# A two-layer graph network on one core: the first group as four tasks, and a new order of steps around the change of layers and in the second layer

## The chip, the cores and the metric

The kernel runs on one core of a Trainium2 chip. The metric is the time of one execution on the device in microseconds (us). Before the change three runs took 2112.41, 2112.71 and 2116.83 us; the median is 2112.71 us. One more execution was profiled.

## The reference

There are 128 graphs of 128 nodes with 512 features, all in float32. Two layers follow each other, each with a residual and a layer norm. Cut to what is computed:

```python
# layer 0, per graph
deg = sum(adj, -1); agg = (adj @ x) / max(deg, 1e-6)
x = layernorm(x + relu(concat([x, agg]) @ W.T))
# layer 1, per graph
Xw = x @ Wv + bv; e = leaky_relu(sj(Xw)[None, :] + si(Xw)[:, None] + ab, 0.2)
T = adj * exp(e);  T = T / (sum(T, -1) + 1e-12)
H = x @ Wk[0] + bk[0] + (T @ x) @ Wk[1] + bk[1] + (T @ T @ x) @ Wk[2] + bk[2]
x = layernorm(x + relu(H))
```

## The kernel before

**Groups and products.** Four graphs make a group, so the left operand of a group has 512 rows and 512 features; there are 32 groups (`NG`) in each layer. The adjacency is applied after the weights: the first layer computes `x @ W` for both halves of `W` and then multiplies one half by the normalised adjacency, and the second layer does the same with the weights of the three hops and two extra columns for the scores. The big product is done by a scheme that needs seven block products where the plain one needs eight, twice nested. One outer product (called 1 to 7) is a sequence of seven inner products of 128x128 by 128x256 (first layer) or 128x385 (second layer). The sums of blocks that it needs are made on the left operand (`x_inner`, `x_s1` to `x_s4`, tiles `xu`, `xl`, `xs`) and on the weights (`w_inner`, `w_outer`, the tile `big`). A matmul in float32 appears in the profile as two MATMUL instructions, called passes here.

**Tasks and steps.** A task is a Python generator that yields after each step; a step issues one inner product (in the first layer's paired tasks two) and what belongs to it. `P12`, `P56`, `P74` and `T` make a group of the first layer, `O1` to `O7` and the combination `C` one of the second. Tasks run on two lanes of four PSUM banks, `bA` and `bB`. Within an outer product, X, Y, W and Z are the four banks of its lane. Step 1 writes X, which ScalarE copies to Y (L617 in the second layer); step 2 writes Z, which is copied to the tile s5 (L623, or L621 with a bias); step 3 adds into X, and VectorE writes W = X + s5 (L626); in adding tasks POOL adds to s5 (L660); step 4 adds into Y, which is evicted (L647 on ScalarE, L656 on VectorE); step 5 adds into X, and VectorE takes X + s5 as a result (L650 or L663); step 6 adds into W, which is evicted; step 7 adds into X once more, which is evicted last. So step 3 waits for the copy of step 1, step 5 for the add of step 3, and step 7 for the direct add of step 5. `O5` starts with a copy of the bias to X (L615).

**The order.** The order of all instructions on every engine is written out by hand. The lists `PA`, `PT`, `PB` and `PL` name the steps of a group of the first layer, of the change of layers, of a group of the second layer and of the last group; a name in small letters belongs to the group before. `PB` is used for all groups of the second layer but the last, the first from its `O5.1` on. Everything that is no step (loads, turns, sums, layer norm, softmax) is an operation with a place: a number in half steps, relative to the start of its group, in `PLACES_A` (first layer), `PLACES_B` (second layer), `PLACES_M` and `PLACES_L` (the end), `PLACES_T` (loads of the second layer's weights) and `START`. An even place is after the step's own instructions, an odd one after its late evictions. Each engine works through its list in order, and SyncE (SP) issues nearly all transfers in order.

**The first group.** At the start the derived weights do not exist yet. The task `first` computes group 0 with 56 inner products in 14 steps of four matmuls, two columns (o = 0, 1), and each step uses both halves of the left operand (`xu`, `xl`). The constants of the second layer's bias and scores are folded (`fold_constants`) between these steps, with the loaded `wvt` in the buffers of the tile `y`. `first_last` (FL) multiplies by the adjacency.

**Layer norm.** The last products of a group are followed by the residual on VectorE (L371), the mean on POOL (`ln_mean`, L488), four squares on ScalarE (`ln_var`, L493), the scales on POOL (`ln_scales`, L499 to L501) and four applications on ScalarE (`ln_apply`, L506).

Of the kernel before, what the change touches and what calls it, by code (L numbers as in the profile page):

```python
# [8 lines left out]
FP = mybir.dt.float32  # L9
# [7 lines left out]
def kernel(  # L17
# [14 lines left out]
    nc = tc.nc  # L32
# [9 lines left out]
    R = 32  # L42
# [67 lines left out]
    wvt_sb = [p2.tile([P, 2, F], FP, name=f"wvt{i}", tag="y") for i in range(2)]  # L110
# [3 lines left out]
    bk_sb = p1.tile([K, F], FP, name="bk_sb", tag="TT")  # L114
# [5 lines left out]
    load_w0([nc.scalar], 1)  # L120
    load_w0([nc.scalar], 3)
    load_adj(0)
    for i in range(2):
        nc.sync.dma_start(wvt_sb[i], wvt[i * FH : (i + 1) * FH, :].rearrange("(c p) f -> p c f", p=P))
# [32 lines left out]
    def fold_constants():  # L157
        ones_row = ones[:].to_broadcast([P, P])
        pb, pc, pw = bB[0], bB[3], bB[0]
# [17 lines left out]
        w2row = p1.tile([2, NC, Q, R], FP, name="w2row", tag="TT")  # L177
# [79 lines left out]
    def x_inner(n, p):  # L257
        need(("x_turn", n, p, 1))
        t = (xu, xl)[p][n]
        left_sums([S_, S_, S_, S_], [t[:, :, i] for i in range(7)])  # L260
# [71 lines left out]
    def p12(lane, g):  # L332
        r, c11 = rs[g], c11s[g] = blocks(p2, "r"), blocks(p2, "c11")

        def evict(b, t):
            L_.copy(part(r, b), t[:, :FH])
            V.tensor_add(part(c11, b), t[:, FH:], part(r, b))
        yield from pair(lane, g, 1, 2, evict)
# [10 lines left out]
    def p74(lane, g):  # L349
        r, c22, c21 = rs[g], blocks(p2, "c22"), blocks(p2, "c21")  # L350
        c22s[g], c21s[g] = c22, c21

        def evict(b, t):
            need(("P56", g, {BY: 4, BWW: 6, BZ: 7, BX: 7}[b]))
            L_.copy(part(c22, b), t[:, :FH])
            V.tensor_add(part(c21, b), t[:, FH:], part(r, b))
            V.tensor_add(part(c21, b), t[:, :FH], part(c21, b))
        yield from pair(lane, g, 7, 4, evict)
# [68 lines left out]
    def first(lane, g):  # L427
        c11, c21 = blocks(p2, "c11"), blocks(p2, "c21")
        c11s[g], c21s[g] = c11, c21

        def column(o, bank_of, evict):
            X, Y, W, Z = [bA[i] for i in bank_of]

            def prod(dst, k, start=False):
                for h in range(2):
                    for i in range(2):
                        mm(dst[:, h * FH : (h + 1) * FH], (xu, xl)[h][g][:, i, LEFT[k]], wf[:, SLOT[2 * i + o], RIGHT[k]],
                           start and i == h == 0)
            s5 = halves()
            prod(X, 1, True)  # L440
            L_.copy(Y, X)
            yield
            prod(Z, 5, True)
            L_.copy(s5, Z)
            yield
            prod(X, 6)
            V.tensor_add(W, X, s5)
            yield
            prod(Y, 2)
            yield  # L450
            prod(X, 7)
            evict(BY, Y)
            V.tensor_add(Z, X, s5)
            yield
            prod(W, 3)
            yield
            prod(X, 4)
            evict(BWW, W)
            evict(BZ, Z)
            late.append((evict, BX, X))  # L460
            yield

        def evict0(b, t):
            L_.copy(part(c11, b), t[:, :FH])
            V.tensor_copy(part(c21, b), t[:, FH:])
        yield from column(0, (0, 1, 2, 3), evict0)

        def evict1(b, t):
            i, h = b
            L_.copy(bB[i][:, h * FH : (h + 1) * FH], t[:, :FH])  # L470
            V.tensor_copy(bB[2 + i][:, h * FH : (h + 1) * FH], t[:, FH:])
        yield from column(1, (1, 2, 0, 3), evict1)
        lane[:] = [bA[2], bA[3], bA[1], bA[0]]

    def first_last(lane, g):
        new_mv(g)
        for p, t in ((1, c21s[g]), (0, c11s[g])):
            for i in range(2):
                b = 2 * p + i
                mm(bB[b], aTs[g][:, b], t[:, i, :, :FH])  # L480
                late.append((residual, g, b, bB[b]))
            yield
        lane[:] = [bB[2], bB[0], bB[1], bB[3]]
# [326 lines left out]
    TASKS = {"F": first, "FL": first_last, "P12": p12, "P56": p56, "P74": p74, "T": last, "O1": o1, "O2": o2, "O5": o5,  # L810
             "O6": o6, "O7": o7, "O4": o4, "O3": o3, "C": combine}
    lanes = [list(bA), list(bB)]
    steps = []

    def step(lane, name, g, k):
        steps.append((lane, name, g, k))

    PA = "p74.5 P12.1 P12.2 p74.6 P12.3 p74.7 P12.4 t.1 P12.5 P12.6 t.2 P12.7 P56.1 t.3 P56.2 t.4 t.5 P56.3 t.6 t.7 t.8 t.9 t.10 t.11 P74.1 P74.2 P56.4 P56.5 P56.6 P74.3 P56.7 P74.4".split()
    PT = "p74.5 O1.1 O1.2 p74.6 O1.3 O1.4 p74.7 t.1 t.2 O1.5 O1.6 O1.7 O2.1 t.3 O2.2 t.4 t.5 O2.3 t.6 t.7 t.8 t.9 t.10 t.11 O2.4 O2.5 O2.6".split()
    PB = ("o3.7 O1.1 O1.2 O2.1 O1.3 O2.2 O1.4 O1.5 O1.6 O1.7 O2.3 O2.4 O5.1 O5.2 O2.5 O5.3 O5.4 O2.6 O5.5 "  # L820
          "O2.7 O6.1 O5.6 O6.2 O5.7 O7.1 O6.3 O7.2 O6.4 O6.5 O7.3 O6.6 O6.7 O7.4 O4.1 O7.5 O4.2 O7.6 O4.3 "
          "O7.7 O4.4 O4.5 O4.6 c.1 O4.7 O3.1 c.2 O3.2 O3.3 O3.4 c.3 c.4 c.5 c.6 c.7 c.8 O3.5 O3.6").split()
# [3 lines left out]
    for k in range(14):  # L826
        step(0, "F", 0, k + 1)
# [18 lines left out]
    for g in range(NG):  # L846
        base[NG + g] = base[NG] + len(PB) * g
        for s in PB[PB.index("O5.1") if g == 0 else 0 :] if g < NG - 1 else PL:
# [16 lines left out]
    def place(n, pos, f, *a):  # L865
        at(2 * base[n] + pos, f, *a)

    PLACES_A = {
# [9 lines left out]
        ("y_store", 0, 1): 280, ("ln_var", 0, 2): 229, ("sum_r", 0, 1): 77, ("load_adj", 0): 129, ("ln_apply", 0, 0): 245,  # L878
        ("ln_apply", 0, 3): 257, ("ln_var", 0, 1): 229, ("load_y", 0, 0): 163, ("x_s2", 1): 71, ("ln_var", 0, 3): 233,
        ("t_load", 0): 125, ("x_turn", 1, 0, 0): 14, ("t_turn", 0): 189, ("sum_r", 0, 0): 85, ("x_turn", 1, 0, 1): 33,  # L880
        ("y_store", 0, 0): 258, ("load_y", 0, 1): 183, ("ln_apply", 0, 2): 270, ("ln_var", 0, 0): 231, ("t_back", 0): 158,
        ("t_exp", 0): 140, ("x_s4", 0): 43, ("ln_mean", 0): 224, ("sum_c", 0, 1): 106, ("ln_scales", 0): 233,
        ("sum_c", 0, 0): 114, ("t_sums", 0): 150, ("x_s3", 1): 84, ("x_s1", 1): 69, ("load_left", 2, 0): 66,
        ("x_turn", 1, 1, 0): 2, ("t_scores", 0): 116, ("t_norm", 0): 151, ("x_inner", 1, 0): 38, ("x_inner", 1, 1): 25,
        ("load_left", 2, 1): 38, ("x_turn", 1, 1, 1): 12, ("ln_apply", 0, 1): 256,
# [20 lines left out]
    for n in range(2 * NG):  # L906
        for (name, dn, *a), pos in (PLACES_A if n < NG else PLACES_B).items():
# [6 lines left out]
            place(n, pos, OPS[name], m - NG if name in OWN else m, *a)  # L914
# [10 lines left out]
    def fold(i):  # L925
        next(folding, None)
# [9 lines left out]
    def w_outer(i):  # L936
        need(("w_inner", 1), *{1: [], 2: [("w_outer", 1)], 3: [("F", 0, 14)], 4: [("w_outer", 2)]}[i])
# [4 lines left out]
        ("w_inner", 1): 9, ("x_s2", 1): 30, ("fold", 2): 3, ("a_turn", 0): 16, ("w_outer", 2): 16, ("fold", 4): 11,  # L942
        ("degree", 0): 10, ("a_norm", 0): 10, ("load_left", 1, 1): 9, ("x_s1", 1): 21, ("fold", 5): 16, ("fold", 3): 8,
        ("w_outer", 1): 11, ("fold", 7): 10, ("fold", 6): 17, ("x_s3", 1): 22, ("w_outer", 4): 19, ("load_y", 0, 0): 17,
# [72 lines left out]
```

## Time and profile before

| what | value |
|---|---|
| median of three runs | 2112.71 us |
| the profiled execution's own time | 2111.64 us |
| its span, first to last instruction | 2109.8 us |
| TensorE busy | 2083.5 us, 7104 MATMUL |
| VectorE, ScalarE, POOL busy | 1464.6, 1145.5, 1539.4 us |
| TensorE idle before the second product of the start | 4.1 us, on the turn of `xl` |
| a group of the first layer | about 24.65 us |
| a group of the second layer | 39.5 us |

The profile comes from one execution. Busy time of TensorE counts every matmul to its modelled end, and matmuls overlap, so a short pause between two of them need not appear as idle time; the distance from start to start tells more. A line of the timeline gives the start, the time from there to the end of the last of the merged instructions, the engine, the line of the source, the operation, its tiles and its shape, how many were merged, and in brackets how long the engine was idle before and what ended that.

### The profile page before, as it was taken

What the parts mean: (1) busy time and instruction counts of PE and PEld (TensorE: products, weight loads), DVE (VectorE), ACT (ScalarE), POOL (GpSimd) and SP (SyncE); (2) the same over time, 40 slices, a digit from 0 to 9 for tenths busy, and PEclk for the clock granted to TensorE, in tenths of its full rate; (3) what the DMA queues carried; (4) which work ended last, traced back from release to release, by engine and by line L of the source; (5) the groups of instructions that cost most, each with busy time, mean ns of one, the idle gap of its engine ahead of it and who ended that gap; (6) DMA issues with size and microseconds to landing.
All of it is one profiled execution on the core that took longest, in us unless ns stands there. A gap on an engine that the chain in (4) does not pass through costs nothing.

```text
span 2109.8 us, 25967 instructions
## 1 busy us (share of the span) xinstructions
PE 2083.5 (99%) x7104; PEld 1328.1 (63%) x7104; DVE 1464.6 (69%) x3235; ACT 1145.5 (54%) x2879; POOL 1539.4 (73%) x1432
## 2 busy tenths in 40 slices
PE   8999999999999999999999999999999999999997
PEld 5887888888778886555555555555555555555553
DVE  4778777777777776666666666666666666666665
ACT  2665666666656665355455455455455455455454
POOL 5877888887767776767767767767767767767763
PEclk9999999999999999999999999999999999999999
DMA  7766666566566768334434434434434434434423
GB/s 177 183 186 190 189 184 173 159 190 192 160 173 182 191 164 239 76 91 121 109 91 119 112 91 121 109 91 120 111 91 120 111 91 120 111 91 121 110 71 115
DMA packets 429486, 287.13 MB, mean 136 GB/s; under 512 B 153497, under 2 KB 352281, under 8 KB 429340
## 3 DMA queue, kind: packets, MB, share of 16 engines
q1 hardware_dynamic: 428092, 283.62, 50.7%
q10 hardware_dynamic: 1120, 1.84, 0.4%
q8 instruction: 56, 0.92, 0.2%
q14 instruction: 90, 0.74, 0.1%
q0 software_dynamic: 128, 0.01, 0.0%
HBM read 191.60 MB, written 93.79 MB: 135 GB/s over the span
## 4 chain that ended last, share of the span: by engine, by line
PE 95%; DVE 2%; POOL 1%; DMA 1%; ACT 1%; issue 0%; ACTq 0%; SPq 0%; POOLq 0%; DVEq 0%
PE bB L149 50%; PE bA L149 45%; DVE y L371 1%; DVE r L663 1%; DMA xb<-in_x_dram 0%; DMA big<-wd 0%; DMA big<-in_w0t_dram 0%; PE bB L174 0%; POOL s L660 0%; ACT junk L493 0%; POOL r L696 0%; ACT T L762 0%; POOL xs L265 0%; POOL xs L269 0%; POOL xu L277 0%
## 5 line engine op out<-in xcount | busy, mean ns | idle before, releaser
L149 PE MATMUL bA<-big,xu 128*128 128x256 f32 (+1 forms) x1834 | 578.6, 435 | 3.3 <-DVE r L663 1.0
L149 PEld LDWEIGHTS bA<-big,xu 128*128 128x128 f32 x1834 | 345.6, 190 | 177.6 <-issue 25.7
L149 PE MATMUL bB<-big,xl 128*128 128x256 f32 (+1 forms) x1330 | 399.1, 416 | 0.2 <-ACT bB L617 0.2
L149 PE MATMUL bA<-big,xs 128*128 128x256 f32 (+1 forms) x1316 | 387.9, 418 | 0.2
L149 PEld LDWEIGHTS bB<-big,xl 128*128 128x128 f32 x1330 | 252.0, 190 | 99.3 <-issue 15.5
L149 PEld LDWEIGHTS bA<-big,xs 128*128 128x128 f32 x1316 | 245.1, 190 | 92.1 <-DVE bA L626 14.3
L149 PE MATMUL bB<-big,xu 128*128 128x256 f32 (+1 forms) x868 | 286.1, 440 | 2.6 <-DVE bB L388 2.5
L149 PE MATMUL bB<-c,TT 128*128 128x512 f32 x512 | 246.3, 594 | 0.0
L660 POOL TENSOR_TENSOR s<-s,r 128x385 f32<-128x385 f32 x128 | 127.6, 997 | 151.2 <-DVE bA L626 105.3
L493 ACT ACTIVATE junk<-y,mv 128x512 bf16<-128x512 f32 x252 | 181.6, 721 | 78.6 <-POOL mv L488 74.5
L149 PEld LDWEIGHTS bB<-big,xu 128*128 128x128 f32 x868 | 159.0, 189 | 91.7 <-DVE r L650 19.3
L506 ACT ACTIVATE y<-y,mv,rstd 128x512 f32<-128x512 f32 x252 | 201.4, 811 | 1.3 <-POOL mv L501 1.3
L626 DVE TENSOR_TENSOR bA<-bA,s 128x385 f32<-128x385 f32 x128 | 72.5, 567 | 165.6 <-ACT s L623 117.8
L149 PE MATMUL bA<-big,xl 128*128 128x385 f32 (+1 forms) x490 | 181.3, 476 | 4.2 <-DVE xl L254 4.1
L371 DVE SCALAR_TENSOR_TENSOR y<-bB,y 128x512 f32<-128x512 f32 x256 | 170.4, 682 | 19.8 <-PE bB L149 13.5
L149 PE MATMUL bB<-big,xs 128*128 128x385 f32 x448 | 173.5, 492 | 0.9 <-POOL xl L242 0.9
L149 PEld LDWEIGHTS bB<-c,TT 128*128 128x128 f32 x512 | 97.2, 190 | 89.4 <-issue 48.6
L797 ACT COPY bB<-r 128x512 f32<-128x512 f32 x64 | 37.7, 589 | 193.4 <-DVE big L796 188.2
L277 POOL TENSOR_TENSOR xu<-xu,xs 128x896 f32<-128x896 f32 x63 | 131.3, 2085 | 10.3 <-PE bA L149 10.3
L149 PEld LDWEIGHTS bA<-big,xl 128*128 128x128 f32 x490 | 93.3, 191 | 71.0 <-DVE c L663 7.9
L273 POOL TENSOR_TENSOR xl<-xu,xl 128x896 f32<-128x896 f32 x63 | 133.3, 2116 | 1.1
L269 POOL TENSOR_TENSOR xs<-xs,xu 128x896 f32<-128x896 f32 x63 | 131.7, 2090 | 2.4
(172 smaller groups left out, 3540.3 us busy)
## 6 DMA issues: line engine op xcount, KB each, us to landing
xb<-in_x_dram SPq DMA_DIRECT2D x256, 128.0 KB, 3.5
y<-in_x_dram SPq DMA_DIRECT2D x64, 512.0 KB, 4.5
yd<-y SPq DMA_DIRECT2D x64, 512.0 KB, 2.8
xb<-yd SPq DMA_DIRECT2D x256, 128.0 KB, 3.9
y<-yd SPq DMA_DIRECT2D x64, 512.0 KB, 4.4
out_dram<-y SPq DMA_DIRECT2D x62, 512.0 KB, 2.8
ag<-in_adj_dram SPq DMA_DIRECT2D x64, 256.0 KB, 4.0
sb<-sd SPq DMA_DIRECT2D x252, 64.0 KB, 3.1
```

The source lines that it names most:

```text
L149: nc.tensor.matmul(dst, lhsT, rhs, start=start, stop=True, skip_group_check=True)
L269: S_.tensor_sub(xs[n][:, 1], xs[n][:, 0], xu[n][:, 0])
L273: S_.tensor_sub(xl[n][:, 0], xu[n][:, 0], xl[n][:, 0])
L277: S_.tensor_sub(xu[n][:, 1], xu[n][:, 1], xs[n][:, 1])
L371: V.scalar_tensor_tensor(y, t, 0.0, y, ALU.max, ALU.add, accum_out=mvs[n][:, b, 0:1])
L493: L_.activation(junk, ys[n, b // 2][:, b % 2], AF.Square, bias=mvs[n][:, b, 0:1], accum_out=mvs[n][:, b, 1:2])
L506: L_.activation(y, y, AF.Identity, bias=mvs[n][:, b, 0:1], scale=rstds[n][:, b : b + 1])
L626: V.tensor_add(W, X, s5)
L660: S_.tensor_add(s5, s5, part(src, BZ, BW))
L663: V.tensor_add(part(dst, BZ, BW), X, s5)
L797: L_.copy(at_[b], row(b, 254, 766, 1))
```

## The change

- The first group is computed by four tasks A to D, one for each column o and half h of the left operand, with seven steps of two products each. A uses `xu` alone and the weights 0 and 2. Each works in halves of four banks (A and B in `bA`, C and D in `bB`); C and D evict to `bA`. Their order is the list `PF`. The turns of `xl` and its sums move to places among these steps, and the inner sums of group 0 go from POOL to VectorE.
- The loads of the weights 1 and 3 are shared by the queues of ScalarE and SyncE. `wvt` is loaded from step 16 on, into the buffers of `c22`. The folding of the constants moves to steps 38 to 51, beside group 1, in banks of `bA`. All places of `START` are new. The lanes start with exchanged banks.
- `PT` is new; the first group of the second layer has its own list `PG`; the others but the last have a new `PB`. `PLACES_B` and `PLACES_T` are new.
- Operations of the last two groups of the first layer and the first two of the second take their places from a new table `PLACES_S`, counted from the start of `PT`.

```diff
-    load_w0([nc.scalar], 1)
-    load_w0([nc.scalar], 3)
+    load_w0([nc.scalar, nc.sync], 1)
+    load_w0([nc.scalar, nc.sync], 3)
     load_adj(0)
...
-        pb, pc, pw = bB[0], bB[3], bB[0]
+        need(("FL", 0, 2))
+        pb, pc, pw = bA[2], bA[3], bA[2]
...
-        left_sums([S_, S_, S_, S_], [t[:, :, i] for i in range(7)])
+        left_sums([S_ if n else V] * 4, [t[:, :, i] for i in range(7)])
...
+    def first(g, o, h):
+        X, Y, W, Z = [t[:, h * FH : (h + 1) * FH] for t in (bA, bB)[o]]
+        if o == 0:
+            dst = blocks(p2, "c21" if h else "c11")
+            (c21s if h else c11s)[g] = dst
+        else:
+            need(("w_inner", 1))
+
+        def prod(dst, k, start=False):
+            for i in range(2):
+                mm(dst, (xu, xl)[h][g][:, i, LEFT[k]], wf[:, SLOT[2 * i + o], RIGHT[k]], start and i == h == 0)
+
+        def evict(b, t):
+            if o == 0:
+                to = part(dst, b)
+            else:
+                need(("FA", 0, 7), ("FB", 0, 7))
+                to = bA[2 * h + b[0]][:, b[1] * FH : (b[1] + 1) * FH]
+            if (b[0] + b[1]) % 2:
+                L_.copy(to, t)
+            else:
+                V.tensor_copy(to, t)
+        s5 = halves()[:, :FH]
...
+        prod(X, 7)
+        V.tensor_add(Z, X, s5)
+        yield
+        prod(W, 3)
+        late.append((evict, BWW, W))
+        yield
+        prod(X, 4)
+        late.append((evict, BZ, Z))
+        late.append((evict, BX, X))
+        yield
...
+    PF = "A.1 A.2 A.3 A.4 A.5 A.6 B.1 B.2 B.3 C.1 B.4 A.7 C.2 B.5 C.3 B.6 B.7 C.4 C.5 C.6 D.1 D.2 D.3 D.4 D.5 D.6 C.7 D.7".split()
-    PT = "p74.5 O1.1 O1.2 p74.6 O1.3 O1.4 p74.7 t.1 t.2 O1.5 O1.6 O1.7 O2.1 t.3 O2.2 t.4 t.5 O2.3 t.6 t.7 t.8 t.9 t.10 t.11 O2.4 O2.5 O2.6".split()
-    PB = ("o3.7 O1.1 O1.2 O2.1 O1.3 O2.2 O1.4 O1.5 O1.6 O1.7 O2.3 O2.4 O5.1 O5.2 O2.5 O5.3 O5.4 O2.6 O5.5 "
-          "O2.7 O6.1 O5.6 O6.2 O5.7 O7.1 O6.3 O7.2 O6.4 O6.5 O7.3 O6.6 O6.7 O7.4 O4.1 O7.5 O4.2 O7.6 O4.3 "
-          "O7.7 O4.4 O4.5 O4.6 c.1 O4.7 O3.1 c.2 O3.2 O3.3 O3.4 c.3 c.4 c.5 c.6 c.7 c.8 O3.5 O3.6").split()
+    PT = "p74.5 p74.6 O1.1 O1.2 O1.3 p74.7 O1.4 t.1 O1.5 O1.6 t.2 O1.7 O2.1 t.3 O2.2 t.4 t.5 O2.3 t.6 t.7 t.8 t.9 t.10 t.11 O2.4 O2.5 O2.6".split()
+    PG = ("O5.1 O5.2 O5.3 O5.4 O2.5 O2.6 O6.1 O6.2 O5.5 O5.6 O5.7 O7.1 O6.3 O6.4 O7.2 "
+          "O6.5 O2.7 O7.3 O6.6 O7.4 O6.7 O4.1 O4.2 O7.5 O4.3 O7.6 O7.7 O4.4 c.1 O4.5 "
+          "O4.6 c.2 c.3 c.4 O4.7 O3.1 O3.2 O3.3 O3.4 c.5 c.6 c.7 c.8 O3.5 O3.6").split()
+    PB = ("O1.1 o3.7 O1.2 O1.3 O2.1 O2.2 O1.4 O1.5 O1.6 O1.7 O2.3 O2.4 O5.1 O5.2 O5.3 O2.5 O2.6 O5.4 O5.5 "
+          "O2.7 O6.1 O5.6 O6.2 O5.7 O7.1 O6.3 O7.2 O6.4 O6.5 O7.3 O6.6 O6.7 O7.4 O4.1 O4.2 O7.5 O4.3 O7.6 "
+          "O4.4 O7.7 O4.5 c.1 c.2 O4.6 O4.7 O3.1 O3.2 c.3 c.4 O3.3 c.5 O3.4 c.6 c.7 c.8 O3.5 O3.6").split()
...
+    def place_op(n, pos, name, m, *a):
+        key = name, m - NG, *a
+        if name not in OWN and key in PLACES_S:
+            at(2 * start_b + PLACES_S[key], OPS[name], m, *a)
+        else:
+            place(n, pos, OPS[name], m - NG if name in OWN else m, *a)
+
+    PLACES_S = {
+        ("ln_apply", -2, 3): 4, ..., ("ln_apply", -2, 2): 10, ..., ("ln_apply", -2, 1): 15, ..., ("ln_apply", -2, 0): 15,
+        ("ln_var", -1, 0): 58, ..., ("ln_scales", -1): 62, ("ln_mean", -1): 48, ("ln_var", -1, 2): 55, ...
+        ("x_inner", 1, 1): 61, ("x_inner", 1, 0): 64, ("x_s4", 0): 80, ("x_s1", 1): 97, ("x_s2", 1): 99, ("x_s3", 1): 127,
+        ...
+    }
...
     PLACES_B = {
-        ("ln_apply", 0, 2): 270, ..., ("ln_apply", 0, 3): 257, ..., ("load_left", 2, 0): 66, ("load_left", 2, 1): 38,
+        ("ln_apply", 0, 2): 274, ..., ("ln_apply", 0, 3): 255, ..., ("load_left", 2, 0): 83, ("load_left", 2, 1): 59,
...
     START = {
+        ("x_turn", 0, 1, 0): 6, ("x_turn", 0, 1, 1): 8, ("x_inner", 0, 1): 13, ("w_inner", 1): 16, ("w_outer", 1): 22,
+        ("load_wvt",): 32, ("a_load", 0): 35, ("a_turn", 0): 59, ("fold", 1): 77, ..., ("fold", 7): 102, ...
```

## The prediction

> **What bounds the kernel now.** I read the page first, then the stretches, TensorE's waits, and the timeline of the start, of the change of layers and of one steady group of the second layer. The page and three stretches (us, then busy us and instructions of PE, PEld, DVE, ACT, POOL, then clock, DMA share, GB/s):
>
> ```profile
> span 2109.8 us, 25967 instructions
> PE 2083.5 (99%) x7104; PEld 1328.1 (63%) x7104; DVE 1464.6 (69%) x3235; ACT 1145.5 (54%) x2879; POOL 1539.4 (73%) x1432
> 0.00:20.00 20.00, 13.21 (x29) 7.31 (x30) 6.84 (x11) 1.85 (x2) 10.14 (x26) 0.91 0.99 216
> 800.00:845.00 45.00, 41.41 (x140) 25.65 (x138) 28.29 (x64) 23.65 (x53) 27.17 (x31) 1.00 0.85 242
> 1100.00:1500.00 400.00, 399.16 (x1153) 213.19 (x1152) 262.79 (x545) 206.09 (x509) 290.05 (x263) 1.00 0.42 107
> ```
>
> TensorE sets the time. Its visible idle time is 26.3 us: most of it in the first 20 us and near 820 us, next to nothing in steady stretches. Its longest waits (total, times, longest):
>
> ```profile
> PE bA L149 <- DVE xl L254: 4.1, 1, 4.1
> PE bB L149 <- DVE bB L388: 2.5, 1, 2.5
> PE bB L149 <- POOL xl L242: 0.9, 1, 0.9
> ```
>
> Busy hides the rest, because a matmul's shown end is modelled. What counts is the distance between starts. A product is two MATMULs; where nothing holds it, four starts of 385 columns take 1.29 us, 0.646 per product. One steady group (start, duration):
>
> ```profile
> 1134.18 2.45 PE L149 MATMUL bA<-big,xu 128*128 128x385 f32 x6
> 1135.09 0.56 DVE L663 TENSOR_TENSOR r<-bA,s 128x385 f32<-128x385 f32 x1
> 1136.46 1.46 PE L149 MATMUL bB<-big,xu 128*128 128x385 f32 x4
> 1137.31 0.46 ACT L617 COPY bB<-bB 128x385 f32<-128x385 f32 x1 [0.22 <-PE bB L149]
> 1139.69 3.02 PE L149 MATMUL bB<-big,xu 128*128 128x385 f32 x8
> 1142.55 1.46 PE L149 MATMUL bA<-big,xu 128*128 128x385 f32 x4
> 1143.29 0.49 ACT L615 COPY bB<-beta 128x385 f32<-128x385 f32 x1
> 1143.92 1.53 PE L149 MATMUL bB<-big,xs 128*128 128x385 f32 x4
> 1145.29 0.81 PE L149 MATMUL bA<-big,xu 128*128 128x385 f32 x2
> 1153.70 1.59 PE L149 MATMUL bA<-big,xs 128*128 128x385 f32 x4
> 1155.13 0.81 PE L149 MATMUL bB<-big,xl 128*128 128x385 f32 x2
> 1171.07 2.81 PE L149 MATMUL bB<-big,TT 128*128 128x512 f32 x6
> 1173.71 2.44 PE L149 MATMUL bA<-big,xu 128*128 128x385 f32 x6
> ```
>
> The group takes 1173.71 - 1134.18 = 39.53 us; its work is 49 x 0.646 + 8 x 0.858 = 38.5. The lost 1.0 us sits in five places. (a) O3.5, O3.6, o3.7: 2.28 us instead of 1.94, 0.34 lost: o3.7 adds into the bank that L663 reads, and L663 is late behind the residuals on DVE. (b) O1.4 to O1.7: 2.86 instead of 2.59, 0.27 lost: O1.7 follows O1.5 with one product between, less than the direct add L650 takes. (c) before and after O5.1's first pass, 0.16: the bias copy L615 is late. (d) O6.4, O6.5: 1.43 instead of 1.29, 0.14: the s5 copy L623 stands behind a layer-norm apply on ACT. (e) c.8: 0.07.
>
> Here the Trainium skill ("Trainium Kernel Development and Optimization", Performance Expectations) calls matmul busy time a bad metric for the distance to the roofline. Read by the busy column, a new step order could win 0.84 us in the 400 us shown, 2.5 us over the second layer; read by starts, 31 us lie there. I go by starts.
>
> **The change, part by part.**
>
> *Start.* The first product ran at 11.25 us, the next waited for the left operand's second half:
>
> ```profile
> 10.79 1.16 DVE L931 TENSOR_TENSOR big<-big 128x512 f32<-128x512 f32 x1 [0.78 <-DMA big<-in_w0t_dram]
> 15.64 1.30 DVE L254 STREAM_TRANSPOSE xl<-xb 128x512 f32<-128x512 f32 x2 [0.82 <-issue]
> 16.41 2.08 PE L149 MATMUL bA<-big,xl 128*128 128x256 f32 x4 [4.13 <-DVE xl L254]
> ```
>
> That is 4.13 us of waiting, and eight passes after it at 0.427 us instead of 0.216 (16.41 to 19.81), another 1.7. Task A needs neither the second half nor weights 1 and 3, so six steps of 4 x 0.216 = 0.86 us fill 11.25 to 16.4. Their cover: four sums of the first half, now on DVE, taken at 0.4 us each (L345 of the same width: 0.41), 9.8 to 11.4; then the weight sums at 0.61 to 0.68 (they took 1.2 beside POOL's sums, 0.61 alone at 28 us), so A.2 starts on time near 12.1. B.1 needs the half that lands at 15.6 as before (the same eight loads stand ahead of it) and its turn, 0.7: 16.4. Then DVE is late: a copy, an add, the second turn and the first sum end near 18.2, while B.1 ends at 17.3: B.2 waits 0.9. B.7 waits some 0.3 more behind the weight sums and w_outer. At 19.8 the old kernel had done 2.6 us of products; the new one has 5.2 + 0.9 + 1.5 = 7.6. Gain 5.0 - 0.3, say 4.5. Bounds: 5.8 if nothing waits; 1 if DVE, or weights 1 and 3 (their last landed at 21.97, behind the wvt loads that now go to step 16), hold C for 3 us. The fold's products are the same, moved beside group 1's; the stretch that held them lost 3.4 us from 20 to 60 us, so 0, bounds 1 either way. SP: wvt, moved past group 1's loads, is used at step 40; the turned adjacency is due at step 35, about 39 us, its load would land near 35. ACT issues ten weight loads instead of fourteen and is free near 10.5 us, not 15.9, with its 1.28 us table load done by 11.8.
>
> *Change of layers.* The 2.48 us wait at 819.64 is t.2 behind L388, which on DVE stands behind four evictions, whose ACT copies L355 stand between four layer-norm applies of 0.81. The new PT puts O1.5 and O1.6 between t.1 and t.2 (1.3 us), O1.1 to O1.3 ahead of p74.7, and two applies after t.1. Counted from p74.5: L355 of the last bank ends at 5.5, its two adds at 6.4, L388 at 6.8; t.2 is due at 6.9. So the wait and its 0.16 of following loss go. The 0.90 before 833.10 is named POOL, but L615, behind a layer-norm square at 831.80 that waited for POOL's mean, ended at 832.99. The squares now come after O5.1: another 1.0 goes. Given back: PG has O5.1 to O5.3 and O5.5 to O5.7 in a row (0.25 each, below), and POOL is full from 846 to 858 us (x_s1, x_s2, x_s3 2.08 each, two row sums 1.82, two adds 1.0), ending at o3.7 (1.17 lost now). x_inner before ln_scales and x_s4 before O7.3's add keep that queue as full; TensorE arriving 1.5 us earlier waits there instead, less one product, since O1.1 now covers o3.7. Gain 2.6 + 1.0 + 0.65 - 0.5 - 0.3 = 3.5. Bounds: 5.5, and -1 if the POOL queue grows by two 2.08 us operations more.
>
> *Steady groups, 30 of them (g 1 to 30; the last keeps its list).* Worked by the new list, zero at O3.5. (a) L663 ends at 1.5, and o3.7 is now due at 1.94: 0.34 gone. (b) stays. (c) stays: L615 still follows O1.7's copy and the apply. (d) The apply moves from before the s5 copy of O6.2 to after it: 0.14 gone; the copies then behind it, O5.7's and O7.1's, end near 20.2, O7.3 is due at 20.6. (e) O3.4 now lies between c.5 and c.6: 0.07 gone. Sum 0.55.
> New: O5.1, O5.2, O5.3 in a row. O5.3 adds into the bank that L617 copies. A copy ends 1.31 after its product starts (O1.1 at 1136.46, copy 1137.31 + 0.46); TensorE went on 0.14 after L615's end (1143.78 to 1143.92); so 1.45 against 1.29: 0.16 lost, and 0.08 to 0.10 in the next pass, as in (a) to (d): 0.25. Behind O5.3 stands all of TensorE. Lower bound 0.07, if the release takes 0.05 as after L663 at 1175.19; upper 0.35.
> Thin cover: O1's s5 copy stands on ACT behind squares 2, 1 and 0 and the score copies: 1.25 + 0.9 (copy of O1.1), + 0.37, + 0.84, + 0.70, + 0.58, copy to 5.1, DVE's L626 to 5.7; O1.5 is due at 5.8. O6.7 is due 0.17 after its L663. O2's second and third sums on POOL, the turns on DVE and the SP loads moved by 3 to 21 places (load_left to steps 29 and 41, 12 to 18 us ahead of the turns; a load lands in 3 to 7) are hidden; without that cover, a late turn would cost its delay in every group.
> Net 0.30 x 30 = 9.0. Bounds: 0.55 - 0.07 + 0.1 of (c) = 0.58, 17 us; and 0.55 - 0.35 - 0.3 (a miss at O1.5 or O6.7 of 0.2 and 0.1 behind it) = -0.1, 3 us lost. I take the middle because each part has a row of its own.
>
> *End.* PL is unchanged, the places around it move by a few steps under 10 to 17 us of slack: 0, bounds 1 either way.
>
> Sum: 4.5 + 3.5 + 9.0 = 17.0 us. The profiled execution took 2111.64 (span 2109.8 and 1.8 around it): 2094.6. Its time lies 1.1 below the median of the three runs, 2112.71, so I say 2095.
>
> **The rivals.**
> 1. *The steady part gives nothing.* O5.3's new wait and a miss at one thin place take the 0.55 back. For it: both margins are under 0.2 us. Against: the removed waits follow from the order alone. 4.5 + 3.5: 2104.
> 2. *More than forecast.* O5.3 waits 0.07, (c) goes too since ACT reaches L615 earlier, the start loses nothing: 5.5 + 5 + 17: 2084.
> 3. *Slower.* ACT at the head of a steady group: if one more 0.84 us square or a late sum on POOL comes ahead of O1's s5 copy, O1.5 waits 0.75 with 0.1 behind it in all 30 groups: 25.5 us lost against 17 won, 2120. It decides from 17 / 30 = 0.57 us of such a wait on. Against: the squares depend on ln_mean, which starts when it did.
> 4. *The change doesn't do what it says:* t.2 and the start stay bound by DVE, steady as forecast: 11 us, 2100; inside the forecast's range.
>
> **How the numbers follow.** Forecast (2089 to 2100, rival 4 within): 0.52. Rival 1 (2100 to 2110): 0.22. Rival 2 (2080 to 2089): 0.14. Rival 3: 0.08 above 2117, and 0.04 between, of partial misses. What this kernel's measurement can tell from no change is about 0.2%, 4.2 us: faster (below 2108.5) is 0.52 + 0.14 + 0.18 of rival 1 = 0.84; same 0.07; slower 0.09. The range 2085 to 2109 leaves out some 0.07 below and 0.12 above.
>
> **What would show it.** Right: no TensorE wait over 1 us between 11 and 20 us; no wait on L388 at the change; steady groups of 39.2 us, with o3.7 0.65 after O1.1 and c.8 on time, and a pause of 0.25 before O5.3. Wrong: a steady group of 39.5 or more; a wait before O1.5; B.2 or C.2 late by more than 2 us; POOL holding o3.7 of the second layer's first group by over 2 us.

## The result and the profile after

The changed kernel takes 2095.61 us (median of four runs, 2094.99 to 2096.49); beside it the kernel before took 2113.29 us (2112.41 to 2116.83). The ratio is 0.9914 with a 95% interval of 0.9896 to 0.9931. The profiled execution took 2095.15 us, its span is 2093.3 us, 16.5 us less than before.

The page and the three stretches of the kernel after, with the columns as before (PE, PEld, DVE, ACT, POOL, clock, DMA share, GB/s):

```profile
span 2093.3 us, 25892 instructions
PE 2076.1 (99%) x7104; PEld 1330.8 (64%) x7104; DVE 1465.6 (70%) x3247; ACT 1154.0 (55%) x2883; POOL 1532.1 (73%) x1424
0.00:20.00 20.00, 17.34 (x53) 10.81 (x54) 9.52 (x19) 3.12 (x6) 3.69 (x18) 1.00 1.03 199
800.00:845.00 45.00, 44.89 (x151) 27.75 (x149) 30.21 (x68) 23.50 (x50) 30.57 (x32) 1.00 0.78 225
1100.00:1500.00 400.00, 399.96 (x1165) 217.15 (x1164) 263.52 (x548) 209.19 (x513) 294.50 (x267) 1.00 0.45 108
```

TensorE's busy time went up by 4.1 us in the first 20 us and by 3.5 us from 800 to 845 us. In the 400 us of steady groups it rose by 0.8 us, but the same window holds twelve more passes: 12 x 0.323 = 3.9 us of work (shorter groups account for nine of the twelve; the rest depends on where the window cuts a group). That is the gain which the busy column hides. Of TensorE's waits (total, times, longest) the three old heads are gone. Of those left behind the warm-up, the 2.2 us stand at the end of the kernel, as before, and so do totals of 0.9 and 0.8 that are not shown:

```profile
PE bB L151 <- ACT T L771: 2.2, 1, 2.2
PE bB L151 <- DVE r L672: 0.5, 1, 0.5
PE bB L151 <- ACT bA L454: 0.4, 1, 0.4
```

The start, in the timeline of the kernel after (lines have moved: the matmul is L151, the warm-up L148, L663 and L650 are now L672 and L659, L617 is L626, L623 is L632, L626 is L635, L615 is L624):

```profile
11.95 5.34 PE L151 MATMUL bA<-big,xu 128*128 128x256 f32 x24
17.13 2.89 PE L151 MATMUL bA<-big,xl 128*128 128x256 f32 x12
26.34 0.92 PE L151 MATMUL bA<-big,xl 128*128 128x256 f32 x3 [0.28 <-DVE bA L473]
36.55 1.13 PE L151 MATMUL bB<-big,xl 128*128 128x256 f32 x4 [0.45 <-ACT bA L454]
```

The 24 passes are the six steps of A; B.1 follows them at once, and B.2 and B.3 follow B.1 with 0.14 us lost at B.2. At the change of layers t.2 (815.06) starts after its add and O5.1 (825.76) after the bias copy, without a wait:

```profile
814.15 0.42 DVE L395 TENSOR_TENSOR bA<-bA,s 128x256 f32<-128x256 f32 x1
815.06 0.59 PE L151 MATMUL bA<-big,xu 128*128 128x256 f32 x2
824.22 0.48 ACT L624 COPY bA<-beta 128x385 f32<-128x385 f32 x1 [4.66 <-DVE y L378]
825.76 3.09 PE L151 MATMUL bA<-big,xs 128*128 128x385 f32 x8
```

One steady group of the second layer, from O3.5 on:

```profile
1125.02 1.46 PE L151 MATMUL bB<-big,xu 128*128 128x385 f32 x4
1125.94 0.56 DVE L672 TENSOR_TENSOR r<-bB,s 128x385 f32<-128x385 f32 x1
1126.32 0.81 PE L151 MATMUL bA<-big,xu 128*128 128x385 f32 x2
1126.96 0.81 PE L151 MATMUL bB<-big,xu 128*128 128x385 f32 x2
1130.20 3.08 PE L151 MATMUL bA<-big,xu 128*128 128x385 f32 x8
1133.11 1.46 PE L151 MATMUL bB<-big,xu 128*128 128x385 f32 x4
1134.49 2.35 PE L151 MATMUL bA<-big,xs 128*128 128x385 f32 x6
1136.68 1.46 PE L151 MATMUL bB<-big,xu 128*128 128x385 f32 x4
```

O3.5 and O3.6 take 1.30, and o3.7 (1126.96) starts 0.64 after O1.1: part (a) is gone. O1.4 to O1.7 take 2.91 instead of 2.59, and O5.1 to O5.3 take 2.19 instead of 1.94.

To see where the time went I took, in both traces, each distance from one start to the next and subtracted the usual one (0.216, 0.323 or 0.429 us for 256, 385 or 512 columns). What is over is TensorE's loss:

| stretch | loss before | loss after | gain | forecast |
|---|---|---|---|---|
| first 100 us | 9.2 | 5.0 | 4.1 | 4.5 |
| 100 us to the change of layers | 4.2 | 4.8 | -0.6 | 0 |
| change of layers (from 2 us ahead of the first 385-column pass to 60 us behind it) | 8.0 | 4.5 | 3.5 | 3.5 |
| second layer up to the last 45 us | 31.1 | 21.3 | 9.8 | 9.0 |
| last 45 us | 5.3 | 6.1 | -0.8 | 0 |

The rows add up to 16.0 of the 16.5 us. The other 0.5 us lies in the eight passes of 128 columns in the last 45 us, which this count leaves out: they lose 0.5 us less than before, so that the end loses 0.3 us and not 0.8. A steady group takes 39.22 us instead of 39.54.

### The profile page after: what moved, and what is told of

It is laid out like the page before. It is cut to its first block, busy times and chain, and to the rows that moved or that the text cites. A ratio compares the mean times of both kernels' runs of the same rounds, so it can differ in the third digit from the quotient of the medians.

```text
span 2093.3 us, 25892 instructions
## 1 busy us (share of the span) xinstructions
PE 2076.1 (99%) x7104; PEld 1330.8 (64%) x7104; DVE 1465.6 (70%) x3247; ACT 1154.0 (55%) x2883; POOL 1532.1 (73%) x1424
## 4 chain that ended last, share of the span: by engine, by line
PE 97%; POOL 1%; DVE 1%; ACT 0%; issue 0%; ACTq 0%; POOLq 0%; DVEq 0%
PE bA L151 51%; PE bB L151 45%; PE bA L148 0%; PE bA L177 0%; POOL s L669 0%; POOL c L713 0%; POOL r L705 0%; PE bB L148 0%; ACT junk L502 0%; POOL xs L272 0%; POOL xs L268 0%; DVE y L378 0%; POOL xu L280 0%; PE bA L187 0%; ACT T L771 0%
## 5 line engine op out<-in xcount | busy, mean ns | idle before, releaser
L151 PE MATMUL bB<-big,xu 128*128 128x385 f32 (+1 forms) x1806 | 562.1, 434 | 0.7 <-DVE r L672 0.5
L151 PEld LDWEIGHTS bB<-big,xu 128*128 128x128 f32 x1806 | 341.8, 190 | 167.7 <-issue 44.8
L151 PE MATMUL bA<-big,xl 128*128 128x256 f32 (+1 forms) x1358 | 405.8, 416 | 0.4 <-DVE bA L473 0.3
L151 PE MATMUL bB<-big,xs 128*128 128x256 f32 (+1 forms) x1316 | 384.1, 416 | 0.0
L151 PEld LDWEIGHTS bA<-big,xl 128*128 128x128 f32 x1358 | 257.2, 190 | 100.6 <-issue 16.0
L151 PEld LDWEIGHTS bB<-big,xs 128*128 128x128 f32 x1316 | 249.1, 190 | 84.7 <-ACT bB L626 6.2
L151 PE MATMUL bA<-big,xu 128*128 128x256 f32 (+1 forms) x896 | 294.3, 440 | 0.4 <-DVE bA L635 0.2
L151 PE MATMUL bA<-c,TT 128*128 128x512 f32 x512 | 242.2, 595 | 0.0
L502 ACT ACTIVATE junk<-y,mv 128x512 bf16<-128x512 f32 x252 | 182.6, 725 | 89.5 <-POOL mv L497 85.3
L151 PEld LDWEIGHTS bA<-big,xu 128*128 128x128 f32 x896 | 162.0, 189 | 95.4 <-DVE r L659 19.3
L151 PE MATMUL bA<-big,xs 128*128 128x385 f32 x448 | 173.8, 499 | 0.1
L151 PE MATMUL bB<-big,xl 128*128 128x385 f32 (+1 forms) x462 | 172.0, 480 | 0.8 <-ACT bA L454 0.4
L635 DVE TENSOR_TENSOR bB<-bB,s 128x385 f32<-128x385 f32 x128 | 72.5, 567 | 121.0 <-PE bB L151 83.2
L151 PEld LDWEIGHTS bA<-c,TT 128*128 128x128 f32 x512 | 97.5, 191 | 89.9 <-issue 48.9
L626 ACT COPY bB<-bB 128x385 f32<-128x385 f32 x128 | 60.2, 470 | 143.8 <-PE bB L151 143.8
```

Of the source, the lines that this page charges most:

```text
L151: nc.tensor.matmul(dst, lhsT, rhs, start=start, stop=True, skip_group_check=True)
L502: L_.activation(junk, ys[n, b // 2][:, b % 2], AF.Square, bias=mvs[n][:, b, 0:1], accum_out=mvs[n][:, b, 1:2])
```

## The experiments

The kernel before ran beside each of the three sets below; its medians there are 2111.91, 2110.89 and 2111.95 us. Each ratio is to the median beside it. The changed kernel did not run in these sets, and the kernel before moved by up to 2.4 us between sets, so a difference from 2095.61 us holds to about 2 us; what ran once is read by its trace.

### The start alone, and the steady groups alone

The changed kernel with the old `PT`, `PB`, `PLACES_B` and `PLACES_T`, without `PG` and `PLACES_S`:

```diff
-        for s in PL if g == NG - 1 else PB if g else PG:
+        for s in PB[PB.index("O5.1") if g == 0 else 0 :] if g < NG - 1 else PL:
...
-    PLACES_S = { ... }
+    PLACES_S = {}
```

> The changed kernel with the old PT, PB, PLACES_B and PLACES_T and without PLACES_S and PG: the four tasks, the moved loads and the moved fold alone. Theory: the 4.1 us wait on xl and the slow passes after it go, some 0.7 us comes back because the warm-up matmuls run slowly for longer in this profile: 4 to 5 us won, 2108.5 to 2109.5; the waits at the change of layers (2.5 and 0.9) and the groups of 39.54 us are back. Rival: part of the gain at the start is paid back by the fold beside group 1 and the transfers that moved, 2 us or less won.

And the kernel before with the new `PB` and `PLACES_B` and nothing else:

> The kernel before with the new PB and PLACES_B alone; the start, PT and the other places are the old ones, and the second layer's first group takes the new PB from O5.1 on. Theory: the five waits fall as forecast whatever happens before, so a steady group takes 39.2 us instead of 39.54, 30 x 0.32 = 9.6 us, and the kernel some 2103.5. Rival, read from the busy column: TensorE is 99.8% busy there, so an order of steps can win at most 0.08 us a group, 2.5 us in all, 2111.

The start alone took 2108.74 us (ratio 0.9985, 0.9976 to 0.9995), inside the range expected, though in medians it won 3.2 us and not 4 to 5. Its loss in the first 100 us is 5.0, its steady group 39.54 us: the 4.1 us of the start stand by themselves.

The new steady order alone took 2105.39 us (0.9969, 0.9956 to 0.9982), 1.9 us more than expected. The steady group is 39.20 us, so the steady gain stands; but the change of layers lost 11.9 us instead of 8.0. The new list runs there into the first group, and TensorE waits once for a direct add behind POOL's queue (start, duration):

```profile
847.75 0.56 DVE L663 TENSOR_TENSOR r<-bA,s 128x385 f32<-128x385 f32 x1 [4.38 <-POOL s L660]
848.36 0.92 PE L149 MATMUL bA<-big,xs 128*128 128x385 f32 x2 [3.10 <-DVE r L663]
849.84 2.77 PE L149 MATMUL bA<-big,xl 128*128 128x385 f32 x4
```

Behind the wait four passes from 849.84 take 2.56 us from start to start instead of 1.29, and a fifth is as slow: the clock was down. In this stretch the row of the windows reads 0.71 for it:

```profile
848.00:852.00 4.00, 3.64 (x8) 2.11 (x9) 2.36 (x5) 0.46 (x1) 3.06 (x3) 0.71 0.28 56
```

So with the old order and places around the change of layers the new steady order pays 3.9 us there, which the changed kernel, with its own `PT`, `PG` and `PLACES_S`, does not; which of the three avoids it was not tested.

### Part (a): o3.7 ahead of O1.1 again

```diff
-    PB = ("O1.1 o3.7 O1.2 O1.3 ...
+    PB = ("o3.7 O1.1 O1.2 O1.3 ...
```

> The changed kernel with O1.1 and o3.7 exchanged at the head of PB, nothing else. Theory: o3.7 again stands straight behind O3.6 and waits for L672, the direct add that is behind the residuals: 0.24 and 0.10 in the next pass, 0.34 x 30 = 10 us lost, 2105.8. Rival: the places of the operations around it won the time, not the order: 2 us or less lost, 2097.

It took 2108.99 us (0.9985, 0.9976 to 0.9995), 3 us more than expected. The steady group is 39.68 us, 0.46 more than after the change. O3.6 to o3.7 loses 0.239 and 0.104 again, the 0.34 of part (a). The rest is an oversight in my expectation: with o3.7 in front, O1.1, O1.2 and O1.3 stand in a row, and O1.3 loses 0.071 and 0.104 for the copy of O1.1, just as O5.3 does behind O5.1; the 0.05 at O1.5 went.

### Rival 3: one more square ahead of O1's s5 copy

```diff
-        ... ("ln_var", 0, 3): 233, ...
+        ... ("ln_var", 0, 3): 231, ...
```

> The changed kernel with one layer-norm square (0.72 to 0.84 us on ACT) two steps earlier in a steady group, so ahead of O1's s5 copy. Rival 3 of the prediction (the cover of O1.5 is thin): O1.5 waits 0.7 to 0.8 more and 0.1 behind it, steady group 40.0 instead of 39.22, 30 x 0.8 = 24 us, 2115 to 2120 us. Against it: the later waits of the same group (before O1.7, O5.1, O5.3: 0.7 in all) shrink when TensorE comes later, so that less than half stays: at most 10 us, 2096 to 2106.

It took 2120.1 us (1.0042, 1.0026 to 1.0058): 24.5 us slower than the changed kernel, slower than the kernel before. The steady group is 40.05 us. The end of the chain in its timeline:

```profile
1135.65 0.46 ACT L632 COPY s<-bA 128x385 f32<-128x385 f32 x1
1136.14 0.57 DVE L635 TENSOR_TENSOR bA<-bA,s 128x385 f32<-128x385 f32 x1 [0.35 <-PE bA L151]
1136.76 0.59 PE L151 MATMUL bA<-big,xu 128*128 128x385 f32 x1 [0.62 <-DVE bA L635]
```

One square more goes ahead of the score copies, the s5 copy L632 follows them, VectorE adds, and O1.5 loses 0.79, with 0.10 in the pass behind it. The later waits did not shrink: they still cost 0.60, as in the changed kernel. The cover of O1.5 was as thin as the prediction had it.

### Part (d): the apply ahead of O6.2's s5 copy again

```diff
-        ... ("ln_apply", 0, 2): 274, ...
+        ... ("ln_apply", 0, 2): 270, ...
```

> The changed kernel with the one layer-norm apply back ahead of O6.2's s5 copy on ACT. The prediction's part (d): O6.5 waits 0.03 and 0.105 behind it, 0.135 in each of 30 groups: steady group 39.35 instead of 39.21, 4 us, 2099 to 2100. Rival: the new order of the steps before it has shifted TensorE against ACT (O5.3 waits there now), so that the apply's place no longer matters: group 39.22, 2095.

The one execution took 2096.11 us, the steady group is 39.21 us: nothing came back. The apply does stand ahead of the copy:

```profile
1143.26 0.81 ACT L515 ACTIVATE y<-y,mv,rstd 128x512 f32<-128x512 f32 x1
1143.97 0.46 ACT L632 COPY s<-bB 128x385 f32<-128x385 f32 x1
1144.46 0.57 DVE L635 TENSOR_TENSOR bB<-bB,s 128x385 f32<-128x385 f32 x1 [2.82 <-ACT s L632]
1144.58 1.46 PE L151 MATMUL bB<-big,xs 128*128 128x385 f32 x4
```

The add ends at 1145.03, and O6.5, the second half of the last line, is due at 1145.22. The old kernel missed this by 0.03 us. The 0.14 of part (d) is gone in the changed kernel, but the apply's place is not what removed it. The new wait of 0.18 at O5.3, which brings TensorE later to this point, is large enough to do it; that is argued, not shown.

### The change of layers: t.2 directly behind t.1, or the applies back

```diff
-    PT = "... O1.4 t.1 O1.5 O1.6 t.2 O1.7 ..."
+    PT = "... O1.4 t.1 t.2 O1.5 O1.6 O1.7 ..."
```

> The changed kernel with t.2 directly behind t.1 in the order around the change of layers, O1.5 and O1.6 behind it; the places of the layer-norm applies stay as changed. Theory (the two steps between cover the chain of four evictions and the add behind them): t.2 is due 1.3 us earlier and waits about 1.2 us for that add, 0.16 lost behind it: 1.0 to 1.4 us lost between 800 and 845 us, 2096 to 2097. Rival (the applies' places alone removed the wait): t.2 waits less than 0.2 us and nothing is lost.

```diff
-        ("ln_apply", -2, 3): 4, ... ("ln_apply", -2, 2): 10, ... ("ln_apply", -2, 1): 15, ... ("ln_apply", -2, 0): 15,
+        ("ln_apply", -2, 3): 3, ... ("ln_apply", -2, 2): 6, ... ("ln_apply", -2, 1): 12, ... ("ln_apply", -2, 0): 10,
```

> The changed kernel with the four layer-norm applies of the first layer's last group at their old places (they stand between the ACT copies that t.2's add waits for, 0.81 us each); the order of the steps stays as changed. Theory: two of the applies come ahead of the last copy again, the add ends 1.6 us later and t.2, which now has some 0.1 to 0.9 us to spare, waits 0.7 to 1.5 us: 2096 to 2097, with the loss between 800 and 845 us. Rival: the order alone removed the wait: t.2 waits less than 0.2 us, nothing lost. Both together would say that either half is enough.

With t.2 behind t.1 (one execution, 2095.78 us) it waits for the add, 0.70 us and not 1.2: counted from p74.5 it is due 0.25 us later, and the add is done 0.15 us earlier, than I had worked out:

```profile
814.05 0.42 DVE L395 TENSOR_TENSOR bA<-bA,s 128x256 f32<-128x256 f32 x1
814.53 0.70 PE L151 MATMUL bA<-big,xu 128*128 128x256 f32 x2 [0.70 <-DVE bA L395]
```

The place loses 0.86, but the whole stretch only 0.5 more (5.0 instead of 4.5), since smaller waits behind it shrink. With the applies back (2094.0 us, one execution) the add was done at 814.78, and t.2 does not wait:

```profile
815.27 0.59 PE L151 MATMUL bA<-big,xu 128*128 128x256 f32 x2
```

The stretch loses 4.1, if anything less than with the changed kernel's places. So the new order of the steps removed the wait alone; the new places of the applies were not needed for it. At their old places the applies hold the copy of O1.1 instead, and O1.3 loses 0.60 us where it lost 0.24, so the expectation was wrong on where they bite. Without the two steps between t.1 and t.2, the rest of the change still took away 1.8 of the 2.48 us.

### The squares of the first group ahead of O5.1 again

```diff
-        ... ("ln_var", -1, 0): 58, ... ("ln_var", -1, 2): 55, ... ("ln_var", -1, 1): 55, ... ("ln_var", -1, 3): 58, ...
+        ... ("ln_var", -1, 0): 60, ... ("ln_var", -1, 2): 60, ... ("ln_var", -1, 1): 54, ... ("ln_var", -1, 3): 51, ...
```

> The changed kernel with the four layer-norm squares of the first group of the second layer ahead of O5.1's copies again (steps 51 to 60 instead of 55 to 58). The prediction's second part of the change of layers: the bias copy stands behind a square that waits for POOL's mean: O5.1 waits 0.5 to 1.0 us with 0.16 behind it, loss around the change of layers 5.1 to 5.6 instead of 4.5, 2095.7 to 2096.3. Rival: the mean starts early enough now, 0 to 0.2.

The one execution took 2098.05 us, the stretch lost 8.8 instead of 4.5: far more than I had said (other stretches of this execution lost 1.4 us less). The chain is the one expected:

```profile
826.83 0.72 ACT L502 ACTIVATE junk<-y,mv 128x512 bf16<-128x512 f32 x1 [7.96 <-POOL mv L497]
827.55 0.47 ACT L624 COPY bA<-beta 128x385 f32<-128x385 f32 x1
828.12 4.52 PE L151 MATMUL bA<-big,xs 128*128 128x385 f32 x8 [2.88 <-POOL xl L245]
```

A square (L502) stands on ScalarE waiting for POOL's mean (L497), the bias copy behind it, and O5.1 behind that. (The profile names POOL's L245, which came at about the same time; L624 ended at 828.02, 0.10 us ahead of the pass. O5.1 does not need L245: in the changed kernel it starts at 825.76 and L245 at 828.07.) The mean waits for the residuals, and TensorE reaches O5.1 some 2 us earlier against them than in the old kernel, so the wait is 2.88 and not 0.9. Part of that is a transfer: VectorE stands idle for 2.25 us ahead of the first residual until its load of `y` has landed (2.47 us in the changed kernel), where in the old kernel it waited 0.43 us for TensorE. Then the clock adds to it: of the eight passes in the last line, four take 0.64 us from start to start instead of 0.32, and the windows show the granted clock:

```profile
828.00:832.00 4.00, 3.88 (x8) 2.07 (x9) 2.08 (x5) 1.22 (x4) 2.14 (x3) 0.62 1.07 355
```

The slow passes lose 1.7 us together. Of the edits tested at the change of layers, moving the squares is thus the most valuable; what it avoids is worth more than what it removed.

### The start: the first sums back on POOL

```diff
-        left_sums([S_ if n else V] * 4, [t[:, :, i] for i in range(7)])
+        left_sums([S_] * 4, [t[:, :, i] for i in range(7)])
```

> The changed kernel with group 0's sums of the left operand back on POOL. The prediction's cover for the start: DVE's sums at 0.42 us each are on time; POOL's take 0.7 to 0.75 us and slow DVE's weight sums beside them (0.69 to 1.2 us). Theory: a step of task A or B waits 0.5 to 1.5 us, loss in the first 100 us 5.5 to 6.5 instead of 5.0, 2096 to 2097. Rival: the six steps of A cover POOL's sums as well, and B.1, which the landing at 15.3 us holds, starts when it did: within 0.3.

The one execution took 2096.85 us; the first 100 us lost 6.0 instead of 5.0. Already A is held: A.3 starts 0.06 us after POOL's L247 ends, and A.5 waits for an add behind VectorE's weight sums, three of which take 1.10 to 1.21 us beside POOL's sums, where each takes 0.69 in the changed kernel. Then B.2 and B.3 wait for POOL:

```profile
12.11 1.17 POOL L247 TENSOR_TENSOR xu<-xu 128x256 f32<-128x256 f32 x1
12.62 1.21 DVE L971 TENSOR_TENSOR big<-big 128x512 f32<-128x512 f32 x1
17.65 0.72 POOL L245 TENSOR_TENSOR xl<-xl 128x256 f32<-128x256 f32 x1 [3.23 <-DVE xl L257]
18.43 1.13 PE L151 MATMUL bA<-big,xl 128*128 128x256 f32 x4 [0.21 <-POOL xl L245]
19.91 1.13 PE L151 MATMUL bA<-big,xl 128*128 128x256 f32 x4 [0.35 <-POOL xl L247]
```

From start to start A's 24 passes lose 0.55 us, B.2 0.47 and B.3 0.62, against 0.14 at B.2 in the changed kernel. The first product came at 11.45 us, 0.5 earlier than there, so of these 1.5 us only 1.0 shows. VectorE's 0.42 us a sum, against POOL's 0.72 and more, is needed for both halves.

### What was left in the steady group

The changed kernel's steady group still lost 0.7 us: 0.05 at O1.5, 0.27 at O1.7, 0.16 around O5.1, 0.18 at O5.3. The next order puts a step of the other lane ahead of O1.7, O5.1 and O5.3:

```diff
-    PB = ("... O1.5 O1.6 O1.7 O2.3 O2.4 O5.1 O5.2 O5.3 O2.5 O2.6 O5.4 O5.5 O2.7 O6.1 ...
+    PB = ("... O1.5 O1.6 O2.3 O1.7 O2.4 O2.5 O5.1 O5.2 O2.6 O5.3 O5.4 O2.7 O5.5 O6.1 ...
...
-        ("t_exp", 0): 139, ... ("ln_apply", 0, 1): 255, ... ("ln_apply", 0, 3): 255, ...
+        ("t_exp", 0): 141, ... ("ln_apply", 0, 1): 257, ... ("ln_apply", 0, 3): 257, ...
```

> The changed kernel with another PB at two places: O2.3 goes between O1.6 and O1.7, O2.5 before O5.1, O2.6 between O5.2 and O5.3, O2.7 between O5.4 and O5.5; the exponential and two applies move by one step with it. Theory: what is left in a group are waits between steps of one outer product: 0.27 before O1.7 and 0.18 before O5.3 go, 0.16 around O5.1 stays: 0.45 x 30 = 13.5 us won, 2082. Rival: the chain from O2's add over x_inner, the softmax sums on POOL and the normalisation on ScalarE to O6.1's copy is as long as the group's products there, so O6.3 waits instead and a group stays at 39.0 or more: 6 us won or less, 2090 or more.

It took 2085.25 us (0.9871, 0.9856 to 0.9886), 10.4 us less than the changed kernel and 3 more than expected. The steady group is 38.89 us; all the old waits but 0.04 at O1.5 are gone, also the 0.16 around O5.1 that I had expected to stay, and a new one stands before O5.7:

```profile
1137.05 0.69 DVE L761 TENSOR_REDUCE rw<-T 128x4 f32<-128x512 f32 x1 [0.95 <-POOL T L759]
1138.55 0.55 DVE L659 TENSOR_TENSOR s<-bA,s 128x385 f32<-128x385 f32 x1
1139.15 0.92 PE L151 MATMUL bA<-big,xs 128*128 128x385 f32 x2
```

O5.5 is now later, and its direct add L659 came behind the reduce of the softmax sums on VectorE, their reciprocal and another eviction; O5.7 loses 0.18, and 0.10 behind it. The next run moves the sums behind that add:

```diff
-        ("t_sums", 0): 150, ... ("t_norm", 0): 151, ... ("x_inner", 1, 0): 36, ...
+        ("t_sums", 0): 152, ... ("t_norm", 0): 153, ... ("x_inner", 1, 0): 38, ...
```

> Against the kernel of the run before it (2085.25 us, steady group 38.891 us). There O5.7 waits 0.28 us (0.18 and 0.10 in the pass behind it) in every steady group, because the direct add of O5.5 stands on DVE behind the reduce of the softmax sums. Theory: with the sums two steps later, behind that add, the wait goes and nothing takes its place: steady group 38.61 us, 30 x 0.28 = 8.4 us, about 2077 us. Rival: the chain behind the sums (reduce, reciprocal, ACT's normalisation) now ends later and holds an ACT copy of O6 in its place: O6.2 or O6.3 waits 0.1 to 0.3, group 38.8 to 39.0, 2082 to 2088 us.

Here the rival held, and more than held: 2091.5 us (0.9904, 0.9887 to 0.992), steady group 39.08 us. O5.7 does not wait, but the later normalisation stands on ScalarE ahead of O6.1's copy:

```profile
1140.33 1.28 ACT L771 ACTIVATE T<-T,rr 128x128 f32<-128x128 f32 x4 [0.31 <-DVE rr L764]
1141.51 0.47 ACT L626 COPY bB<-bB 128x385 f32<-128x385 f32 x1
1142.03 0.91 PE L151 MATMUL bB<-big,xs 128*128 128x385 f32 x2 [0.20 <-ACT bB L626]
```

O6.3 loses 0.37, and 0.10 behind it. The last run moves the normalisation behind the copies, and the apply that stood there behind the next ones:

```diff
-        ("t_norm", 0): 153, ... ("ln_apply", 0, 2): 274, ...
+        ("t_norm", 0): 158, ... ("ln_apply", 0, 2): 280, ...
```

> The order of steps of the 2085.25 us run (steady group 38.891 us, of which 0.28 is O5.7's wait), with the softmax sums two steps later, behind O5.5's direct add, and what comes out of them moved behind the copies that waited for it in the 2091.5 us run: ACT's normalisation (1.28 us) from ahead of O6.1's copy to behind O6.2's s5 copy, and the layer-norm apply that stood there (0.82 us) to behind the next s5 copy. Theory (the waits go where ACT and DVE put a softmax or layer-norm operation ahead of a copy that TensorE needs next): neither O5.7 nor O6.3 waits, steady group 38.6 us, about 30 x 0.28 = 8.5 us below 2085.25: 2077. Rival: the wait moves once more, to O7.3 (its copy now stands behind the normalisation) or to the turned softmax (its store starts 2 us later): group 38.8 or more, 2083 or more.

It took 2077.02 us (2076.31 to 2077.63; ratio 0.9836, 0.982 to 0.9853): 18.6 us less than the changed kernel, 34.9 less than the kernel before beside it. The steady group is 38.61 us, and 0.08 of it is lost. The order that does it:

```profile
1135.18 0.56 DVE L659 TENSOR_TENSOR s<-bA,s 128x385 f32<-128x385 f32 x1
1135.66 0.68 DVE L761 TENSOR_REDUCE rw<-T 128x4 f32<-128x512 f32 x1
1136.48 0.47 ACT L626 COPY bB<-bB 128x385 f32<-128x385 f32 x1
1137.26 0.48 ACT L632 COPY s<-bB 128x385 f32<-128x385 f32 x1
1137.63 1.28 ACT L771 ACTIVATE T<-T,rr 128x128 f32<-128x128 f32 x4
```

Add before reduce on VectorE, both copies before the normalisation on ScalarE. In the 400 us window it has 1183 passes where the changed kernel has 1165, with TensorE shown busy for 400.00 against 399.96 us.

## Why the prediction was right, and where not

2095 us was forecast, and 2095.61 measured. The sum of 17.0 us was made of parts that hold one by one, with the corrections below. That the total came so close is in part luck: the start gave 0.4 us less than forecast, the stretch behind it lost 0.6 and the end 0.3, and the second layer gave 0.8 more.

**Start, 4.5 forecast, 4.1 measured.** That six steps of A fill the time up to the second half is what the trace shows. Of the 0.9 us before B.2 only 0.14 appeared: TensorE came to B.1 at 17.13 us, not at 16.4, because its first product ran at 11.95 us and not at 11.25, and VectorE's first sum of the second half ended at 17.96, not 18.2. Where the first product came as early as forecast (11.16 us, in the run of the start alone), B.2 still lost only 0.19, but A.2, said to be on time, lost 0.41 and B.1 0.25. B.7 shows 0.28 us of idle time, forecast as 0.3, and costs 0.54 from start to start. D.7 at 36.55 (0.45 us idle for a copy on ScalarE, 0.71 from start to start) was not in the sum. The run with the sums on POOL lost 1.0 us more at the start.

**Change of layers, 3.5 forecast, 3.5 measured.** Both waits are gone. The step on t.2 was right in its price, but it gave both edits the credit; one, the order of the steps, is enough. The step on the squares was right in its mechanism, and its price was too small for the new order: 0.9 us is what the old kernel lost, 2.88 us and 1.7 us of slow clock is what the new one would lose. o3.7 of the first group loses 0.69 us instead of 1.17 (0.65 less was forecast, with some given back). The rows in `PG` lose 0.34 at O5.3 and 0.27 at O5.7 with the pass behind, priced 0.25 each; O4.7 loses 0.47 where the old kernel lost 0.24, about the 0.3 that was set aside.

**Steady groups, 0.30 forecast, 0.32 measured per group.** (a), 0.34: right, and shown by its return. (b) 0.27 and (c) 0.16 stayed, as forecast. (e) 0.08 went. (d) went, but the reason given, the apply's place, is not the reason: its 0.14 was right by luck. O5.3's new wait was priced 0.25 and costs 0.18. The prediction let TensorE go on 0.14 us after the end of the copy L626, as it does after the bias copy (L615, now L624); measured, O5.3 starts 0.05 us after it, the lower bound. O1.5 is covered by 0.1 as worked out (VectorE's add ends 0.11 us ahead of it), and yet its second pass starts 0.05 late. These two sizes, 0.07 less and 0.05 more, are the whole error.

**End, 0 forecast,** lost 0.8 by the table and 0.3 with the passes of 128 columns, and the stretch from 100 us to the change of layers 0.6. Both lie inside bounds of 1; no run looks for their cause. The latter stretch lost 4.1 to 4.6 in the eleven other profiles with the new start, so that at least 0.2 of it belongs to that one execution.

**The rivals.** Rival 3 was priced 25.5 us from a wait of 0.75 and 0.1; built, it cost 24.5, or 0.83 per group. It did not decide because the squares stayed behind the s5 copy, by one step. Rival 1 needed O5.3 and O1.5 to lose 0.55; they lose 0.23. Of rival 2, (c) did not go by itself. It went in the last three runs: as many steps stand there between O1.7 and O5.1, but O1.7 comes 0.47 us later, its copy no longer stands waiting behind the apply, and the bias copy L624 ends 0.22 us ahead of O5.1 (2085.25 us run).

## What to carry to other kernels

Read a bound TensorE from start to start: here a group of 39.2 us that looked 100% busy still held 0.7 us, and the runs took 0.6 of it out. For every step that adds into a bank, write down the chain of copy and add that it waits for and what stands ahead of each link on its engine's queue; a wait costs its length and once more about 0.1 us in the pass behind it, times the groups. When a stall is removed, look for the next operation ahead of that queue: moving the softmax sums gave a wait to ScalarE's copies that cost more than the one removed, until the normalisation was moved too.

## What was not expected of the hardware

**Pauses of about 3 us were followed by slow passes.** The wait of 2.48 us (the kernel before, at 819.64 us) was followed by passes at full speed; after waits of 2.88 and 3.10 us four to five passes took 0.64 us instead of 0.32, beginning 0.7 to 1.5 us after the restart, with the granted clock at 0.62 and 0.71 over 4 us. Each time it added 1.6 to 1.7 us. After the 4.13 us at the old start the next eight passes took 3.40 us instead of 1.73, slow from the restart on. The Trainium skill ("TensorE: Matmul & The Clock Gate", Why this matters for your kernels) says that no idle gap between matmul bursts should be over some 3 us; here 2.88 was already enough.

**The warm-up takes a different time in each execution.** In the fourteen profiles of this study the same 16 warm-up passes start at 2.65 us, four to seven of them take over 0.6 us (most 0.85, the first 1.01) instead of 0.43, and the first real product starts between 11.16 and 12.66 us. With the new start part of this is absorbed, because B.1 needs a half that lands at 15.3 us anyway: with the first product at 11.16, 11.95 and 12.66 us, B.1 starts at 16.90, 17.13 and 17.84. The loss in the first 100 us lies between 4.8 and 5.7 us, the latter with the start at 12.66; only the run with the sums on POOL lost more. The Trainium skill (the same page, Part 1) says that the window which opens the clock runs freely, so that the number of slow passes varies from run to run; the traces agree in the varying number (four to seven), and do not show the window.

**The pass after a wait is slow as well.** Where the first pass of a product waited, its second started 0.075 to 0.105 us late in every steady group of every run here. At O1.5, and at c.8 in the kernel before, the second started 0.04 to 0.08 late though the first had not waited. The prediction took this from the trace of before; it is more than half of what O5.3's wait costs (0.105 behind 0.072).
